# One sequence of lists for the horizontal pass, with the work between them in pieces

## The chip, the core and the metric

The kernel runs on one core of a Trainium2 chip. Five engines work side by side, each from its own queue: TensorE (PE; its weight loads are shown apart as PEld), VectorE (DVE), ScalarE (ACT), GpSimd (POOL), and SyncE (SP), which only issues DMAs here. ScalarE and GpSimd issue DMAs too. The metric is device microseconds of one execution, smaller is better.

## What is computed

The input is an image of 256 channels and 64 x 64 pixels. It goes through a group norm, a linear attention over windows, causal attention with a small feed-forward net, and a layer of experts. The change touches the first part and the layer norm that follows it:

```python
q = sigmoid(Wq x); k = sigmoid(Wk x); v = Wv x     # per pixel; 8 heads of 32
v = v / max(norm(v), 1e-12)
outs = []
for w in (1, 2, 4):
    ws = 64 // w                                   # windows of 64, 32, 16 pixels a side
    wk  = box_sum(k, ws)                           # over the window of each pixel
    wkv = box_sum(outer(k, v), ws)
    attn = einsum('bdhw,bdfhw->bfhw', q, wkv)
    norm = einsum('bdhw,bdhw->bhw', q, wk)
    outs.append(attn / (norm + 1e-6))
x = x + Wout concat(outs) + bout
# then, for the 4096 tokens: layer norm, causal attention, feed-forward net, experts
```

## The kernel before

The windows are not summed. With q and k as keys and queries, each pixel's product with the keys of its window is a masked score, so TensorE computes scores against blocks of 128 keys, a mask (bias) pushes scores outside the window to at most zero, a ReLU drops them, and a second product multiplies by v. The whole is done twice, for groups of four heads (`hg` 0 and 1, function `window_heads`), and in two passes each. The **vertical** pass takes key blocks beside a column strip of the image, the **horizontal** pass key blocks above and below a row strip `Y` (0 to 7; 8 image rows, 512 pixels). Keys wholly inside a window come as sums, not scores: `states` builds them on VectorE, `inside` multiplies them by q on TensorE (L410).

Work comes in **parts**: some rows of a strip times the columns that one key block can reach. `packed` fills **lists** of parts with at most 512 columns, the width of a PSUM buffer, and splits a part between two lists only if at least 96 columns go into the first. Before, each row strip is packed by itself, so its last list may be short.

`push` (one list) is the inner step. It takes four PSUM buffers of six, one for each head; TensorE adds the mask (L349, bf16) and the scores (L358) of every part for the four heads, which lie in four groups of 32 rows of the array. Then four evacuations with a ReLU write `pm` (L327 on ScalarE, L329 on VectorE; of eight in turn, ScalarE takes the 1st, 3rd, 5th, 6th and 8th). Then `add` accumulates the list *before* into `acc` (L391): pm times v. When the last part of a strip and a window size is in, `finish` makes `y`: VectorE adds `ov`, the vertical pass's result, which SyncE loads from memory (L667), and GpSimd multiplies by the inverse norm `rn` (L426); for the smallest window VectorE multiplies alone (L422).

Around the lists of a strip Y stands, behind the list with the index given in the loop's `if`s:

- index 1: `spread_norms`, three products of 32 rows (L474), each copied by ScalarE to `rn` (L477);
- index 2: `boxes(Y + 1)`, GpSimd's window sums for the next strip's norms (L441 to L454);
- index 3: `convolve(Y - 1)`, the output projection of the strip before, twelve matmuls (L505) into two PSUM buffers, each added to the tokens `t` by VectorE (L510);
- second group only, index 4: `measure`, the statistics of four token tiles on VectorE; index 5: `norm`, ScalarE's square root and VectorE's reciprocal and four normalisations; index 7: `turn`, eight transposes (L845), a copy by each of VectorE and ScalarE (L846), and two sums (L847);
- third list from the end: `norms`, three products (L462), ScalarE's copy with the epsilon (L465) and four reciprocals on VectorE (L467).

The order of TensorE and GpSimd is that of the program, by `manual_schedule`. The order of VectorE, ScalarE and SyncE is chosen by the scheduler when the kernel is built, from priorities and its own costs. Behind the second group come the last convolution and norm, the causal attention and the experts, which the change leaves as they are.

Of the kernel before, what the change touches and what calls it, by code (L numbers as in the profile page):

```python
# [19 lines left out]
P = 128  # L20
D = 256
# [83 lines left out]
def packed(parts):  # L105
# [3 lines left out]
    while parts:  # L109
        part = parts.pop(0)  # L110
        if part.size <= room:
            out[-1].append(part)
            room -= part.size
            continue
        rows = room // (part.c1 - part.c0)
        if rows * (part.c1 - part.c0) >= 96:
            first, rest = part.split(rows)
            out[-1].append(first)
            parts.insert(0, rest)
        else:  # L120
            parts.insert(0, part)
        out.append([])
        room = 512
# [54 lines left out]
def window_attention(tc, a, t, eps5, ident, causal, first):  # L178
# [5 lines left out]
    with ExitStack() as ctx:  # L184
# [99 lines left out]
        with tc.manual_schedule(engines={mybir.EngineType.PE}):  # L284
# [3 lines left out]
            causal.measure(7)  # L288
            xns = causal.norm(7, w)
            causal.values(1, psum)  # L290
            causal.values(2, psum)
            causal.turn(7, xns, psum)


def window_heads(tc, a, t, ident, hg, norm, raws, load, psum, pools, tables, consts, late, causal):
# [35 lines left out]
    accs, left, state, ys, waiting = {}, {}, {}, {}, []  # L331

# [72 lines left out]
    def inside(group, acc):  # L405

        wi, Y = group
        for X in range(8):
            for h, hs in enumerate(hss):
                nc.tensor.matmul(  # L410
                    acc.rearrange("p (y x) -> p y x", x=HW)[hs, :, 8 * X : 8 * X + 8],
                    lhsT=state["st"][wi][hs, X, :], rhs=q[hs, 8 * Y : 8 * Y + 8, 8 * X : 8 * X + 8],
# [3 lines left out]
    def finish(group, acc):  # L416
# [3 lines left out]
        rn = state["rn"][wi]  # L420
        if wi == 0:
            nc.vector.tensor_mul(o, acc, rn)  # L422
        else:
            view = lambda s: s.rearrange("p (y b x) -> p y b x", b=8, x=8)
            nc.vector.tensor_add(view(o), view(acc), state["ov"][wi].rearrange("p b (y x) -> p y b x", x=8))  # L425
# [32 lines left out]
    def norms(boxed):  # L458

        pn = psum()  # L460
        for wi, box in enumerate(boxed):
            nc.tensor.matmul(pn[32 * wi : 32 * wi + 32, :], lhsT=sums, rhs=box.rearrange("p y x -> p (y x)"),  # L462
                             start=True, stop=True, skip_group_check=True)
        r = sm.tile([96, 512], F32, name="r", bufs=1)
        nc.scalar.activation(r, pn[0:96, :], AF.Identity, bias=eps6[0:96, :])  # L465
        for j in range(4):
            nc.vector.reciprocal(r[:, j * P : (j + 1) * P], r[:, j * P : (j + 1) * P])  # L467
        return r

    def spread_norms(r):  # L470
        rns = []
        for wi in range(3):
# [6 lines left out]
        return rns  # L479

    def states(Y):


        out = [None]
        for wi in (1, 2):
            n = HALF[wi] // 8
            rows = state["h"].tile([P, 9, 32], F32, name="srows")
            nc.vector.tensor_sub(rows, ikv[:, min(8, Y + n), :, :], ikv[:, max(0, Y - n + 1), :, :])
            st = state["h"].tile([P, 8, 32], F32, name=f"st{wi}")
            if n == 2:  # L490
                nc.vector.tensor_copy(st[:, 0, :], rows[:, 2, :])
                nc.vector.tensor_sub(st[:, 1:7, :], rows[:, 3:9, :], rows[:, 0:6, :])
                nc.vector.tensor_sub(st[:, 7, :], rows[:, 8, :], rows[:, 6, :])
            else:
                nc.vector.tensor_copy(st[:, 0:4, :], rows[:, 4:8, :])
                nc.vector.tensor_sub(st[:, 4:8, :], rows[:, 8:9, :].to_broadcast([P, 4, 32]), rows[:, 1:5, :])
            out.append(st)
        return out

    def convolve(Y):  # L500
        for j in range(2):
            pt = psum()
            for i in range(2):
                for n, wi in enumerate((2, 1, 0)):
                    nc.tensor.matmul(  # L505
                        pt[:, i * D : (i + 1) * D], lhsT=ys[wi, Y][:, (2 * j + i) * P : (2 * j + i + 1) * P],
                        rhs=wo[:, n, :], start=(n == 0), stop=(n == 2),
                    )
            td = t[:, 4 * Y + 2 * j : 4 * Y + 2 * j + 2, :]
            nc.vector.tensor_add(td, td, pt.rearrange("p (i d) -> p i d", i=2))  # L510
# [79 lines left out]
    with tc.manual_schedule(engines={mybir.EngineType.PE, mybir.EngineType.Pool}), ExitStack() as keys:  # L590
        with ExitStack() as vctx:
# [25 lines left out]
            for m in range(4):  # L617
# [9 lines left out]
                kp = turned(m)  # L627
            for m in range(4):
# [24 lines left out]

            for i, parts in enumerate(lists[1:]):
                push(parts)
                if i == len(lists) - 4:
                    r = norms(boxed)
            lists = [packed(part for wi in range(3) for part in above(wi, Y)) for Y in range(8)]
            for each in lists:
                expect(each)  # L660
            push(lists[0][0])
        h = state["h"] = keys.enter_context(tc.tile_pool(name="l0h", bufs=1, side="right", reuse_waits="tile"))
        for Y in range(8):
            ov = [None]
            for wi in (1, 2):
                o = h.tile([P, 8, HW], F32, name=f"ov{wi}")
                nc.sync.dma_start(out=o, in_=oscratch[wi].rearrange("b p (y x) -> y p b x", x=HW)[Y])  # L667
                ov.append(o)
            st = states(Y)
            if hg and Y == 7:  # L670
                causal.load()
            for i, parts in enumerate(lists[Y]):
                if (Y, i) != (0, 0):
                    push(parts)
                if i == 2 and Y < 7:
                    boxed = boxes(Y + 1)
                if i == 1:
                    state.update(st=st, ov=ov, rn=spread_norms(r))
                if i == 3 and Y:
                    convolve(Y - 1)  # L680
                if hg and i == 4 and Y:
                    causal.measure(Y - 1)
# [648 lines left out]
```

## Time and profile before

| | us |
|---|---|
| median of 3 runs | 1993.42 (1993.35 to 1994.79) |
| the profiled execution | 1994.53 |
| its span, first to last instruction | 1992.8 |
| vertical pass, first group | about 91 to 202 |
| horizontal pass, first group | about 202 to 511 |
| vertical pass, second group | about 570 to 682 |
| horizontal pass, second group | about 682 to 1009 |
| causal attention and experts | about 1009 to 1993 |

In a line of the timeline stand: start in us from the span's start, duration in us, engine, line, operation, what is written and what is read, shapes (for a matmul the rows and columns of the array, then the operand), how many instructions are merged into the row, and in brackets the idle time of the engine before it and what ended that. An fp32 matmul is recorded as two passes, so four heads with one part are eight records. In a line of a table by stretches stand: the stretch, its length, the busy time and number of instructions of each engine, the granted clock of TensorE (PEclk, 1 is full), the share of the DMA engines and the GB/s.

### The profile page before, as it was taken

The page shows a single profiled execution, that of the slowest core. Times are in us where ns is not written, and L with a number is a line of the kernel's source. Part 1 is how long each engine was busy: PE and PEld are TensorE (multiplying, and loading weights), DVE is VectorE, ACT ScalarE, POOL GpSimd, SP SyncE. Part 2 cuts the span into 40 slices and gives each one's busy share as a digit, 9 for nine tenths or more (in the row PEclk, how much of TensorE's full clock was granted, in tenths as well). Part 3 has the DMA queues.
Part 4 walks back from the last instruction along what each step waited for, and adds up shares of the span by engine and source line. Part 5 has one row for each costly group of instructions (what it writes and reads, how often), then busy time and mean ns, then how long its engine had stood idle before and what let it go on. Part 6 is the DMA issues. An engine that isn't in the chain of part 4 may idle for free.

```text
span 1992.8 us, 46271 instructions
## 1 busy us (share of the span) xinstructions
PE 1859.6 (93%) x20326; PEld 1218.4 (61%) x20326; DVE 1000.5 (50%) x2190; ACT 777.4 (39%) x1331; POOL 431.8 (22%) x709
## 2 busy tenths in 40 slices
PE   4999999999999999999999999999999999879998
PEld 2655565555665555555575656665666666657777
DVE  4644555544554565555663444554553655443343
ACT  1566444444456644444414233233333234223322
POOL 1384323232155123333110000000000000031220
PEclk9999999999999999999999999999999999879999
DMA  7211100000331100000100000000000000010000
GB/s 242 82 52 45 29 13 18 13 18 12 104 92 40 45 18 18 13 13 13 50 2 0 1 0 1 0 1 0 1 0 1 0 1 0 1 43 22 21 22 22
DMA packets 66890, 53.34 MB, mean 27 GB/s; under 512 B 37568, under 2 KB 56792, under 8 KB 66688
## 3 DMA queue, kind: packets, MB, share of 16 engines
q1 hardware_dynamic: 57296, 31.87, 5.8%
q10 hardware_dynamic: 8128, 14.67, 2.1%
q0 software_dynamic: 1264, 3.84, 0.6%
q8 instruction: 159, 2.61, 0.6%
q14 instruction: 43, 0.35, 0.1%
HBM read 32.93 MB, written 17.44 MB: 25 GB/s over the span
## 4 chain that ended last, share of the span: by engine, by line
PE 42%; DVE 6%; ACT 3%; issue 1%; POOL 0%; ACTq 0%; DVEq 0%; POOLq 0%
PE po L1001 11%; PE pa L957 10%; PE ph L1265 6%; PE py L1285 6%; PE pt L987 2%; PE pm L1058 1%; PE acc L391 1%; PE pm L1068 1%; DVE lnst L704 1%; PE ps L505 1%; DVE sT L990 1%; PE ps L358 1%; DVE nbs L965 1%; PE pm L916 1%; ACT s L970 1%
## 5 line engine op out<-in xcount | busy, mean ns | idle before, releaser
L327 ACT ACTIVATE pm<-ps 128x512 f32<-128x512 f32 (+19 forms) x734 | 362.4, 558 | 348.4 <-issue 194.1
L329 DVE TENSOR_SCALAR pm<-ps 128x512 f32<-128x512 f32 (+23 forms) x442 | 267.6, 636 | 315.7 <-PE ps L358 234.5
L391 PE MATMUL acc<-pm,vh 128*32 128x248 f32 (+22 forms) x3424 | 218.5, 356 | 16.8 <-DVE pm L329 16.7
L358 PE MATMUL ps<-q,kh 32*128 32x248 f32 (+23 forms) x3424 | 204.8, 354 | 0.0
L957 PE MATMUL pa<-k,qT 128*128 128x512 f32 (+3 forms) x416 | 180.2, 574 | 7.1 <-ACT qT L918 5.6
L349 PE MATMUL ps<-table,table 32*128 32x192 bf16 (+19 forms) x2512 | 143.1, 261 | 24.4 <-ACT rn L477 8.4
L990 DVE COPY sT<-pt 128x512 f32<-128x512 f32 (+3 forms) x144 | 92.7, 644 | 142.9 <-PE pt L987 142.7
L391 PEld LDWEIGHTS acc<-pm,vh 128*32 128x32 f32 x3424 | 87.3, 110 | 108.5 <-issue 60.8
L349 PEld LDWEIGHTS <-table 32*128 32x128 bf16 x2512 | 50.0, 92 | 162.5 <-issue 155.7
L358 PEld LDWEIGHTS ps<-q,kh 32*128 32x128 f32 x3424 | 142.6, 188 | 7.3 <-issue 2.5
L426 POOL TENSOR_TENSOR y<-y,rn 128x512 f32<-128x512 f32 x32 | 41.3, 1290 | 449.5 <-DVE y L425 297.9
L959 ACT ACTIVATE s<-pa,v 128x512 f32<-128x512 f32 (+3 forms) x112 | 73.8, 661 | 152.1 <-PE pa L957 151.9
L957 PEld LDWEIGHTS pa<-k,qT 128*128 128x128 f32 x416 | 75.7, 191 | 89.3 <-issue 72.4
L965 DVE TENSOR_REDUCE nbs<-s 128x1 f32<-128x512 f32 (+4 forms) x120 | 77.6, 652 | 80.4 <-ACT s L959 59.1
L1285 PE MATMUL py<-w,hT 128*128 128x256 f32 x512 | 111.8, 379 | 0.0
L1001 PE MATMUL po<-kh,sT 128*128 128x257 f32 x406 | 102.8, 395 | 8.7 <-DVE sT L990 8.5
L1285 PEld LDWEIGHTS py<-w,hT 128*128 128x128 f32 x512 | 97.3, 190 | 15.7 <-issue 1.9
L391 PE MATMUL acc<-pm,v 128*32 128x192 f32 (+11 forms) x1600 | 98.5, 360 | 3.9 <-DVE pm L329 2.4
L358 PE MATMUL ps<-q,k 32*128 32x192 f32 (+11 forms) x1600 | 98.4, 359 | 0.0
L1001 PEld LDWEIGHTS po<-kh,sT 128*128 128x128 f32 x406 | 74.7, 195 | 22.4 <-DVE sT L990 13.2
L505 PE MATMUL ps<-l0wo,y 128*128 128x256 f32 x384 | 87.0, 383 | 0.0
L948 POOL MEMSET s<- 128x32 f32 x20 | 2.5, 124 | 376.4 <-PE pt L987 348.4
(304 smaller groups left out, 2899.0 us busy)
## 6 DMA issues: line engine op xcount, KB each, us to landing
oscratch<-ov ACTq DMA_DIRECT2D x32, 256.0 KB
ov<-oscratch SPq DMA_DIRECT2D x32, 256.0 KB
t<-in_xT SPq DMA_DIRECT2D x32, 128.0 KB
vscratch<-v SPq DMA_DIRECT2D x32, 128.0 KB
vh<-vscratch SPq DMA_DIRECT2D x16, 256.0 KB
raw<-in_x SPq DMA_DIRECT2D x7, 512.0 KB
raw<-in_x ACTq DMA_DIRECT2D x7, 512.0 KB
out<-y SPq DMA_DIRECT2D x7, 512.0 KB
```

Source lines behind the costliest of these rows:

```text
L327: nc.scalar.activation(dst, src, AF.Relu)
L329: nc.vector.tensor_scalar_max(dst, src, 0.0)
L349: nc.tensor.matmul(got[h][:, spot].rearrange("p (y x) -> p y x", y=part.r1 - part.r0), lhsT=spread[hs, int(part.vertical), :], rhs=bias[hs ...
L358: nc.tensor.matmul(got[h][:, spot].rearrange("p (y x) -> p y x", y=part.r1 - part.r0), lhsT=keys[hs], rhs=q[hs, part.r0 : part.r1, part.c0 ...
L391: nc.tensor.matmul(out, lhsT=v, rhs=pm[:, h, spot].rearrange("p (y x) -> p y x", y=part.r1 - part.r0), start=fresh, stop=(left[key] == 0), ...
L505: nc.tensor.matmul(pt[:, i * D : (i + 1) * D], lhsT=ys[wi, Y][:, (2 * j + i) * P : (2 * j + i + 1) * P], rhs=wo[:, n, :], start=(n == 0), ...
L957: nc.tensor.matmul(pp[:, 0:m], lhsT=qTs[g][:, c, i * P - g * 512 : n - g * 512], rhs=x[b // 512][c][:, 0:m], start=(c == 0), stop=(c == DC ...
L965: nc.vector.tensor_reduce(nbs[:, at : at + 1], s[:, b : b + m], AX.X, ALU.max)
L990: nc.vector.tensor_copy(sT[:, 0:full], pt[:, 0:full])
L1001: nc.tensor.matmul(acc, lhsT=sT[0:m, j * P : (j + 1) * P], rhs=rhs, start=(b == 0), stop=(m != P))
L1265: nc.tensor.matmul(ph, lhsT=w1v[:, e, c, f, :], rhs=x2[g][c], start=(c == 0), stop=(c == DC - 1))
L1285: nc.tensor.matmul(py, lhsT=hT[:, e, f, j * P : (j + 1) * P], rhs=w2v[:, e, f, :], start=(e + f == 0), stop=(e == 1 and f == FC - 1))
```

## The change

Six things are changed together.

1. A split of a part is allowed from 40 columns on, not 96. This holds for both passes.
2. The horizontal pass is packed as one sequence over all eight strips, so a list may hold the end of one strip and the start of the next.
3. The work around the lists is cut into pieces, and a table `between` puts one piece (sometimes two) behind each list: of the norms one product step, four single reciprocals and three single spreading products, each behind a list of its own; the window states by window size; the convolution in two halves; statistics and norm in two halves, with the square root as a step of its own (`root`); the transposes by channel half, their sums four lists later (`sum_up`).
4. `turn` copies both halves on ScalarE.
5. VectorE and ScalarE keep program order too, from the first vertical list to the end of the horizontal pass of each group.
6. The norms of strip 0 start eight lists before the end of the vertical pass, not three.

```diff
@@ packed
-        if rows * (part.c1 - part.c0) >= 96:
+        if rows * (part.c1 - part.c0) >= 40:
@@ window_heads: norms, spread_norms -> norms
+    strips = [{"st": [None], "ov": [None], "rn": []} for _ in range(8)]
-    def norms(boxed):
-        pn = psum()
...
-        for j in range(4):
+    def norms(boxed, rns):
+        r = sm.tile([96, 512], F32, name="r", bufs=1)
+        def sum_up():
+            pn = psum()
+            for wi, box in enumerate(boxed):
+                nc.tensor.matmul(pn[32 * wi : 32 * wi + 32, :], lhsT=sums, rhs=box.rearrange("p y x -> p (y x)"),
+                                 start=True, stop=True, skip_group_check=True)
+            nc.scalar.activation(r, pn[0:96, :], AF.Identity, bias=eps6[0:96, :])
+        def invert(j):
             nc.vector.reciprocal(r[:, j * P : (j + 1) * P], r[:, j * P : (j + 1) * P])
-        return r
-    def spread_norms(r):
-        rns = []
-        for wi in range(3):
+        def spread_out(wi):
             pn = psum()
             nc.tensor.matmul(pn, lhsT=spreadh[32 * wi : 32 * wi + 32, :], rhs=r[32 * wi : 32 * wi + 32, :],
                              start=True, stop=True)
             rn = state["h"].tile([P, 512], F32, name=f"rn{wi}")
             nc.scalar.copy(rn, pn)
             rns.append(rn)
+        return [sum_up] + [lambda j=j: invert(j) for j in range(4)], [lambda wi=wi: spread_out(wi) for wi in range(3)]
...
+            keys.enter_context(tc.manual_schedule(engines={mybir.EngineType.DVE, mybir.EngineType.Activation}))
...
+            steps, spreads = norms(boxed, strips[0]["rn"])
             for i, parts in enumerate(lists[1:]):
                 push(parts)
-                if i == len(lists) - 4:
-                    r = norms(boxed)
-            lists = [packed(part for wi in range(3) for part in above(wi, Y)) for Y in range(8)]
-            for each in lists:
-                expect(each)
-            push(lists[0][0])
+                if i >= len(lists) - 9 and steps:
+                    steps.pop(0)()
+            lists = packed(part for Y in range(8) for wi in range(3) for part in above(wi, Y))
+            expect(lists)
+            push(lists[0])
...
+        def plan(at, *tasks):
+            for n, task in enumerate(tasks):
+                between.setdefault(at + n, []).append(task)
+            return at + len(tasks)
...
         for Y in range(8):
+            at, after = firsts[Y], firsts[Y + 1]
+            plan(at, lambda Y=Y: (outer(1, Y), outer(2, Y)))
+            plan(at + 1, *(lambda wi=wi, Y=Y: strips[Y]["st"].append(inner(wi, Y)) for wi in (1, 2)))
+            if Y == 0:
+                plan(at + 1, *spreads)
+            if Y < 7:
+                plan(at, lambda Y=Y: ahead(Y + 1))
+                end = plan(max(after - 5, at + 6), *(lambda n=n, Y=Y: got[Y + 1][0][n]() for n in range(5)))
+                plan(max(end, after + 1), *(lambda n=n, Y=Y: got[Y + 1][1][n]() for n in range(3)))
+            if Y:
+                end = plan(at + 3, *(lambda j=j, Y=Y: convolve(Y - 1, j) for j in range(2)))
+                if hg:
+                    g = Y - 1
+                    end = plan(end, *(lambda j=j, g=g: causal.measure(g, (2 * j, 2 * j + 1)) for j in range(2)))
+                    plan(end - 1, lambda g=g: causal.root(g))
+                    end = plan(end, *(lambda j=j, g=g: xns.update({(g, j): causal.norm(g, w, (2 * j, 2 * j + 1))})
+                                      for j in range(2)))
+                    plan(end, *(lambda c=c, g=g: causal.turn(g, xns[g, 0] + xns[g, 1], psum, c) for c in range(DC)))
+                    plan(end + 4, *(lambda c=c, g=g: causal.sum_up(g, c) for c in range(DC)))
+        if hg:
+            plan(firsts[7], causal.load)
+        for n, parts in enumerate(lists):
+            if n:
+                push(parts)
+            for task in between.pop(n, []):
+                task()
@@ Causal.turn
-            (nc.scalar.copy if c else nc.vector.tensor_copy)(self.x[g][c], pt)
+        self.nc.scalar.copy(self.x[g][c], pt)
```

`firsts[Y]` is the first list whose first part is of strip Y (0, 9, 20, 33, 46, 59, 72, 84; the whole has 93). `outer` issues the two loads of `ov` on SyncE, `ahead` GpSimd's box work, `inner` is one window size of the former `states`.

## The prediction

> **What bounds the kernel now.** First the head of the page: which engine fills the span. Then the busy times of the two horizontal passes (one for each group of four heads), which the change rebuilds. Then the timeline there, list by list.
>
> ```profile
> span 1992.8 us, 46271 instructions
> ...
> PE 1859.6 (93%) x20326; PEld 1218.4 (61%) x20326; DVE 1000.5 (50%) x2190; ACT 777.4 (39%) x1331; POOL 431.8 (22%) x709
> ```
>
> ```profile
> core 0: us, PE busy (x) PEld busy (x) DVE busy (x) ACT busy (x) POOL busy (x), PEclk, DMA share, GB/s
> ...
> 202.00:511.00 309.00, 293.40 (x5579) 178.49 (x5578) 157.38 (x274) 140.22 (x285) 88.35 (x106) 0.99 0.08 18
> ...
> 682.00:1009.00 327.00, 302.81 (x5626) 185.82 (x5618) 195.24 (x385) 145.28 (x298) 87.19 (x101) 0.98 0.09 22
> ```
>
> TensorE is the bound; VectorE is at 51% and 60%, ScalarE at 45%, so neither is a limit by its sum. But a busy TensorE is not one at its peak, so I go by starts of matmuls. An unhindered list:
>
> ```profile
> 996.31 0.40 PE L349 MATMUL ps<-table,table 32*128 32x47 bf16 x12
> ...
> 997.63 1.00 PE L391 MATMUL acc<-pm,vh 128*32 128x141 f32 x16
> ...
> 998.57 0.40 PE L349 MATMUL ps<-table,table 32*128 32x192 bf16 x8
> ...
> 999.76 0.71 PE L391 MATMUL acc<-pm,vh 128*32 128x47 f32 x16
> ```
>
> Bias and scores of two parts with 512 columns take 1.19 us (998.57 to 999.76); 487 columns in three parts, the first of 47, take 1.32 us. Going through all 294 lists of the timeline in this way, an unhindered list costs 1.19 us less 2.1 ns for each column short of 512, plus 0.075 us for each part beyond two; its accumulation 0.14 us plus 1.67 ns a column. So an empty list would still cost about 0.25 us. What exceeds this is stall. Three kinds stand out:
>
> ```profile
> 391.25 3.38 DVE L467 RECIPROCAL r<-r 96x128 f32<-96x128 f32 x4 [1.15 <-ACT r L465]
> ...
> 393.09 0.51 PE L391 MATMUL acc<-pm,vh 128*32 128x189 f32 x4
> ...
> 395.19 0.99 PE L391 MATMUL acc<-pm,vh 128*32 128x189 f32 x12 [1.59 <-DVE pm L329]
> 396.11 0.37 PE L349 MATMUL ps<-table,table 32*128 32x192 bf16 x8
> ```
>
> Four reciprocals run as one block ahead of an evacuation; the accumulation takes 3.02 us (393.09 to 396.11), not 0.93.
>
> ```profile
> 400.24 1.13 PE L474 MATMUL ps<-r,spreadh 32*128 32x512 f32 x6
> ...
> 401.39 1.56 ACT L477 COPY rn<-ps 128x512 f32<-128x512 f32 x3 [1.02 <-PE ps L474]
> ...
> 402.03 0.35 PE L349 MATMUL ps<-table,table 32*128 32x192 bf16 x5 [0.57 <-ACT rn L477]
> ```
>
> Three spreading products take three of six PSUM buffers; the next list waits for ScalarE's copy.
>
> ```profile
> 854.28 0.21 PE L349 MATMUL ps<-table,table 32*128 32x93 bf16 x2
> ...
> 854.53 1.38 DVE L836 TENSOR_SCALAR xn<-t,stats 128x256 f32<-128x256 f32 x4
> ...
> 856.56 0.38 PE L349 MATMUL ps<-table,table 32*128 32x93 bf16 x9 [1.55 <-DVE pm L329]
> ```
>
> In the second group the tokens' norm stands ahead of an evacuation: the list takes 3.52 us, not 1.30.
>
> **What goes.** (a) The reciprocals: 14 accumulations over their price by 1.3, 1.9, 2.8, 2.5, 2.1, 2.6, 2.1 us in the first group and 1.3, 1.9, 2.1, 2.1, 2.9, 3.4, 2.1 in the second: 31.2 us; twice 1.37 us more at the end of the vertical passes: 34 in all. One reciprocal (0.85 us) with one list's evacuations (0.65 or 1.3 us) fits into the list's 2.2 us. (b) The wait behind the spread: 16 x 0.82 = 13.2 us. (c) The norm block: 0.97, 2.22, 2.23, 2.22, 0.95, 2.23, 2.34: 13.2 us. (d) Other lists over their price: 24 us, partly in the wake of (a), partly one-part lists (13 a group; a single part of 329 columns is 0.31 us over) too short to cover ScalarE's two evacuations in a row. Together 85 us.
>
> Part of (a) and (c) is clock. The column PEclk:
>
> ```profile
> 306.00:309.40 3.40, 3.40 (x34) 1.52 (x34) 0.25 (x1) 0.00 (x0) 0.00 (x0) 0.51 0.00 0
> ```
>
> Five such windows (from 306, 350, 811, 883 and 931 us) each follow such a stall within 3 us, and cost about 1.5 us each (the list at 307.6 against the like one at 790.8): 7.5 of the 85 us. [...]
>
> What stays: two of three (ScalarE does a list's first two evacuations in every second list, 1.1 us in a row) still wait. A list after such a one is 0.21 to 0.31 us late where no other TensorE work lies between. By the plan 21 lists of the first group's horizontal pass and 17 of the second's have none: 38 x 0.27 = 10 us. New waits: ScalarE's square root now stands in order behind the statistics, VectorE's y behind its evacuations. Seven strips with 0.3 us would be 2 us; 0.25 us in all 186 horizontal lists would be 46; nothing below zero, since an in-order piece cannot shorten a list. I take 8, nearer the low end, because VectorE is at 60% and a late piece falls mostly on a list in which it has one evacuation. So stalls fall from 85 to 18: **-67 us**.
>
> **What comes.** Packing: the parts go from 100 + 214 to 121 + 242 a group, the lists from 46 + 101 to 45 + 93 (worked out from the rule of the packing; columns unchanged). Parts beyond two in a list rise by 58: x 0.075 x 2 groups = 8.7 us; small first and last pieces some 4 to 5 us more (the 47-column list above is 0.1 over); 9 lists x 0.25 x 2 = -4.5. Together **+9**. [...] 72 evacuations fewer (about 0.17 us fixed cost each, from 0.25 us at 94 and 0.59 at 512 columns) are off the path.
>
> Spreading: three products in three row groups run together, 0.97 us from the accumulation's end to the next bias (the list gap 1.84 us against 0.87 without). One behind each list, each costs that alone, since its neighbours need the same row groups or all rows: 2 x 0.97 x 16 strips = **+31 us**. If the first bias of the next list overlapped it, 25; not below.
>
> Convolution and transposes in two pieces each: one more entry and exit, 0.2 us, x 14 and x 7: **+4**.
>
> Moved at no cost: VectorE's window states (1.2 and 2.0 us) come at the lists that also have a spread, which gives them 3.2 us; without that cover 0.5 us a strip. GpSimd's box work (12 us a strip) starts two lists earlier, behind the product of the last y, and is needed eight lists (about 20 us) later; if it were late, the sums wait for it. SyncE's loads of ov are issued behind the strip's first list, wait as before for the last use of the buffer, and are needed nine lists later; the parameters' 14 loads go ahead of the last pair on that queue, which had 20 us to spare. ScalarE's copy of a spread waits for GpSimd's y product of the strip before, done two lists earlier. The second group's input loads still stand between the last evacuations. Everything after the tokens' layer keeps its order; taking x's copy from VectorE to ScalarE (0.69 against 0.58 us) is off the path.
>
> **Sum.** -67 + 9 + 31 + 4 = -23 us. The profiled execution took 1994.5 us (span 1992.8 and 1.7 around), 1.1 above the median of 1993.4; from the median: 1971.
>
> **Rivals.** *Head-of-line waits* (slower): in program order ScalarE and VectorE must sit out each piece's TensorE product before the next list's evacuation. For it: ScalarE's sequence is now evacuate, wait for the spread or statistics, copy, evacuate. Against: TensorE has the same order, so the piece is done before the next scores. The additions are fixed at 44 us, so beside the 10 us that stay it decides from (85 - 44 - 10)/186 = 0.17 us a list on; at 0.21 us the time is 2001. Chance 0.15. *The evacuation stays the limit*: six PSUM buffers at four a list; (d)'s waits return in most lists after two ScalarE evacuations, also where I count a cover, 0.12 us on average: 1985, 0.20. *Draw*: 0.15 to 0.19 us a list, 1993, 0.08. That the pieces do not land between lists is excluded by the order of the built instructions: one reciprocal between two lists' evacuations.
>
> **Numbers.** Forecast 0.57 (1961 to 1980: from no new waits with packing at 6, to 17 us of them). About 0.2% is what a measurement here can tell from no change. Faster 0.57 + 0.20 = 0.77, same 0.08, slower 0.15. Range 1961 to 1998, which leaves out 0.05 below and 0.13 above.
>
> **What would show it.** Right: no list with over 1 us of stall; single reciprocals between evacuations; spreads at about 0.97 us each, three a strip; half-clock windows in the passes gone; horizontal passes near 302 and 309 us instead of 309 and 327. Wrong: a first horizontal pass of 309 us or more; waits of TensorE for rn or stats; a three-part list that costs no more than one of two parts.

## The result, and the profile after

The changed kernel takes 1963.91 us, the median of four runs (1957.54 to 1964.60), against 1994.11 us of the kernel before in its runs. The ratio is 0.9838 with a 95% interval from 0.9822 to 0.9854: 30 us faster by the medians and 32 by the ratio, where the forecast was 23. The profiled execution took 1963.31 us. Its page says that TensorE is still the bound, now with more matmuls (22286, not 20326) and with less room between them:

```profile
span 1961.6 us, 50126 instructions
...
PE 1867.7 (95%) x22286; PEld 1272.9 (65%) x22286; DVE 1013.5 (52%) x2154; ACT 780.3 (40%) x1295; POOL 438.8 (22%) x709
```

The table by stretches has the two horizontal passes in its first two rows, then the two vertical ones, and last the 3.4 us in which the kernel before ran at half clock (PEclk 0.51). A vertical pass is cut at its first mask product, a horizontal one at the last list ahead of the first spread. The first group's horizontal pass ends where TensorE starts on the second group's projections (2.1 us of idle time ahead of that are in it, 3.1 before), the second's with the last accumulation:

```profile
205.60:504.50 298.90, 295.53 (x6090) 196.41 (x6087) 168.12 (x263) 140.66 (x266) 89.94 (x104) 1.00 0.09 21
672.80:976.90 304.10, 302.74 (x6139) 201.52 (x6135) 196.21 (x363) 148.03 (x284) 88.92 (x99) 1.00 0.10 24
93.00:205.60 112.60, 110.16 (x2593) 73.28 (x2593) 51.15 (x80) 68.39 (x133) 74.32 (x129) 1.00 0.14 48
560.00:672.80 112.80, 110.09 (x2593) 73.33 (x2593) 50.68 (x80) 68.34 (x133) 55.62 (x121) 1.00 0.14 47
306.00:309.40 3.40, 3.28 (x87) 2.36 (x88) 2.72 (x4) 1.69 (x4) 0.00 (x0) 1.00 0.00 0
```

Cut in the same way, the passes of the kernel before are 309.5, 325.4, 113.0 and 113.4 us. The horizontal passes became 10.6 and 21.3 us shorter, the vertical ones 0.5 and 0.6: 33.0 us in all, where the two spans differ by 31.2. So the whole result lies in the passes. No half-clock window is left in the passes (PEclk 1.00; there were five in the horizontal passes).

What TensorE waited for shows it most briefly. The view of waits gives: what waits, what it waits for, us in total, times, the longest. In the kernel before, the rows of the passes were

```profile
PE acc L391 <- DVE pm L329: 19.1, 20, 1.6
...
PE ps L349 <- ACT rn L477: 8.4, 16, 0.6
PE ps L349 <- DVE pm L329: 8.2, 7, 1.6
...
PE ps L349 <- ACT pm L327: 5.2, 21, 0.4
```

that is, 40.9 us for evacuations and for the spread's copy (a wait shows only where the engine is idle). In the changed kernel the same rows are

```profile
PE ps L353 <- DVE pm L332: 0.8, 2, 0.4
...
PE ps L353 <- ACT pm L330: 0.3, 1, 0.3
```

and the wait for `rn` is gone. The reciprocals now stand one by one between two evacuations, here in VectorE's timeline:

```profile
227.78 0.94 DVE L475 RECIPROCAL r<-r 96x128 f32<-96x128 f32 x1
228.88 0.69 DVE L332 TENSOR_SCALAR pm<-ps 128x512 f32<-128x512 f32 x1 [0.16 <-PE ps L362]
229.48 0.94 DVE L475 RECIPROCAL r<-r 96x128 f32<-96x128 f32 x1
231.41 1.28 DVE L332 TENSOR_SCALAR pm<-ps 128x506 f32<-128x506 f32 x2 [0.98 <-PE ps L362]
```

And the price of spreading one at a time, in TensorE's timeline:

```profile
315.45 1.03 PE L395 MATMUL acc<-pm,vh 128*32 128x144 f32 x24
316.41 0.69 PE L479 MATMUL ps<-r,spreadh 32*128 32x512 f32 x1
316.42 0.66 PE L353 MATMUL ps<-table,table 32*128 32x217 bf16 x7
316.94 0.59 PE L479 MATMUL ps<-r,spreadh 32*128 32x512 f32 x1
316.95 0.21 PE L353 MATMUL ps<-table,table 32*128 32x69 bf16 x2
...
317.59 1.14 PE L362 MATMUL ps<-q,kh 32*128 32x217 f32 x19
318.66 1.07 PE L395 MATMUL acc<-pm,vh 128*32 128x155 f32 x24
```

The product's two fp32 passes start at 316.41 and 316.94, and mask products start in between. Most of the scores (19 of 24 records) start only from 317.59 on. From one accumulation's start to the next, lists with a spread are about 0.9 us longer than like ones without, over some 100 lists of this trace.

### The profile page after: what moved, and what is told of

It is laid out like the page before. It is cut to its first block, busy times and chain, and to the rows that moved or that the text cites. A ratio compares the mean times of both kernels' runs of the same rounds, so it can differ in the third digit from the quotient of the medians.

```text
span 1961.6 us, 50126 instructions
## 1 busy us (share of the span) xinstructions
PE 1867.7 (95%) x22286; PEld 1272.9 (65%) x22286; DVE 1013.5 (52%) x2154; ACT 780.3 (40%) x1295; POOL 438.8 (22%) x709
## 4 chain that ended last, share of the span: by engine, by line
PE 43%; DVE 6%; ACT 3%; issue 1%; POOL 0%; ACTq 0%; DVEq 0%; POOLq 0%
PE po L1035 12%; PE pa L991 10%; PE ph L1299 6%; PE py L1319 6%; PE pt L1021 2%; PE pm L1092 1%; PE acc L395 1%; PE pm L1102 1%; PE ps L362 1%; PE ps L507 1%; DVE sT L1024 1%; DVE nbs L999 1%; DVE lnst L731 1%; PE pm L950 1%; ACT s L1004 1%
## 5 line engine op out<-in xcount | busy, mean ns | idle before, releaser
L330 ACT ACTIVATE pm<-ps 128x512 f32<-128x512 f32 (+24 forms) x690 | 358.4, 584 | 330.6 <-PE ps L362 176.8
L332 DVE TENSOR_SCALAR pm<-ps 128x512 f32<-128x512 f32 (+21 forms) x414 | 265.3, 668 | 265.2 <-PE ps L362 172.7
L362 PE MATMUL ps<-q,kh 32*128 32x217 f32 (+27 forms) x3872 | 213.1, 336 | 0.0
L395 PE MATMUL acc<-pm,vh 128*32 128x217 f32 (+27 forms) x3872 | 199.7, 329 | 0.0
L362 PEld LDWEIGHTS ps<-q,kh 32*128 32x128 f32 x3872 | 161.2, 185 | 9.7
L353 PE MATMUL ps<-table,table 32*128 32x184 bf16 (+36 forms) x2904 | 142.7, 245 | 5.4 <-issue 1.2
L395 PEld LDWEIGHTS acc<-pm,vh 128*32 128x32 f32 x3872 | 98.0, 109 | 71.7 <-issue 37.1
L430 POOL TENSOR_TENSOR y<-y,rn 128x512 f32<-128x512 f32 x32 | 40.9, 1277 | 432.8 <-DVE y L429 358.2
L353 PEld LDWEIGHTS <-table 32*128 32x128 bf16 x2904 | 57.0, 92 | 108.4 <-issue 97.6
L362 PE MATMUL ps<-q,k 32*128 32x192 f32 (+30 forms) x1936 | 102.8, 337 | 0.0
L395 PE MATMUL acc<-pm,v 128*32 128x192 f32 (+30 forms) x1936 | 95.9, 326 | 0.6 <-issue 0.6
```

What stands on the lines that cost most here:

```text
L330: nc.scalar.activation(dst, src, AF.Relu)
L332: nc.vector.tensor_scalar_max(dst, src, 0.0)
L353: nc.tensor.matmul(got[h][:, spot].rearrange("p (y x) -> p y x", y=part.r1 - part.r0), lhsT=spread[hs, int(part.vertical), :], rhs=bias[hs ...
L362: nc.tensor.matmul(got[h][:, spot].rearrange("p (y x) -> p y x", y=part.r1 - part.r0), lhsT=keys[hs], rhs=q[hs, part.r0 : part.r1, part.c0 ...
L395: nc.tensor.matmul(out, lhsT=v, rhs=pm[:, h, spot].rearrange("p (y x) -> p y x", y=part.r1 - part.r0), start=fresh, stop=(left[key] == 0), ...
```

## Experiments

All times are medians, the ratio is to the kernel before, with its interval. Single runs of the kernel before range from 1985.44 to 1998.05 us, so the four passes of the profiled execution (vertical and horizontal of the first group, then of the second, cut as above) are the finer measure. They come from one trace of each kernel. Where kernels share a pass's code, some agree in it to 0.2 us (the vertical passes of the kernel before and in program order), others only to 1.1 or 2.6 us (the first of threshold 96 and old packing, the second of the last two rows), so a difference of 1 or 2 us in a sum says little. Stalls "over the price" are a list's time less the list price of the prediction.

| kernel | us | ratio | four passes, us | sum |
|---|---|---|---|---|
| before | 1994.11 | 1 | 113.0 + 309.5 + 113.4 + 325.4 | 861.3 |
| changed | 1963.91 | 0.9838 (0.9822 to 0.9854) | 112.5 + 298.9 + 112.8 + 304.1 | 828.3 |
| reciprocals in a block | 1973.88 | 0.9888 (0.9870 to 0.9907) | 116.4 + 301.9 + 116.4 + 308.4 | 843.1 |
| norms in one step | 1997.89 | 1.0027 (1.0010 to 1.0044) | 115.9 + 304.3 + 117.3 + 324.3 | 861.8 |
| scheduler's order | 2001.20 | 1.0027 (1.0016 to 1.0038) | 117.1 + 305.3 + 117.0 + 324.9 | 864.3 |
| before, program order | 1977.55 | 0.9908 (0.9890 to 0.9926) | 113.0 + 309.7 + 113.5 + 311.6 | 847.8 |
| same, norms earlier | 1971.50 | 0.9895 (0.9873 to 0.9917) | 113.0 + 304.4 + 113.5 + 305.8 | 836.7 |
| same, block apart | 1983.08 | 0.9954 (0.9938 to 0.9970) | 111.4 + 309.5 + 111.9 + 315.4 | 848.2 |
| threshold 96 | 1961.68 | 0.9838 (0.9821 to 0.9855) | 109.7 + 301.7 + 109.4 + 305.8 | 826.6 |
| old packing | 1959.96 | 0.9839 (0.9818 to 0.9860) | 110.8 + 300.6 + 109.8 + 306.1 | 827.3 |
| spreads together | 1949.32 | 0.9773 (0.9755 to 0.9792) | 112.3 + 290.8 + 112.7 + 296.3 | 812.1 |
| evacuations in turn | 1952.12 | 0.9788 (0.9768 to 0.9807) | 110.0 + 295.7 + 110.0 + 302.2 | 817.9 |
| the three together | 1924.98 | 0.9653 (0.9631 to 0.9674) | 106.7 + 285.4 + 109.1 + 291.0 | 792.2 |
| spreads under the convolution | 1914.06 | 0.9616 (0.9591 to 0.9641) | 106.8 + 281.2 + 106.5 + 287.9 | 782.4 |

The theory was the prediction's: stalls went because VectorE's and ScalarE's work comes in pieces between evacuations. The rivals: the program order did it, or the packing with fewer lists did.

**Reciprocals in a block again** (the vertical pass's steps likewise):

```diff
-                end = plan(max(after - 5, at + 6), *(lambda n=n, Y=Y: got[Y + 1][0][n]() for n in range(5)))
+                end = plan(max(after - 5, at + 6), lambda Y=Y: got[Y + 1][0][0](), lambda Y=Y: [got[Y + 1][0][n]() for n in range(1, 5)])
```

> The changed kernel, but the four reciprocals of a strip's norms stand in one piece again, behind one list; everything else stays in pieces and in program order. Theory (pieces): TensorE's stalls went because VectorE no longer has 3.4 to 3.8 us of reciprocals ahead of an evacuation. Then 16 accumulations come 1.3 to 3.4 us late again, on average 2.1 us as in the kernel before: +34 us, about 1998 us (1985 to 2003), with accumulations of 2 to 4 us in the timeline. Rival (order): the program order of VectorE and ScalarE did it, and a block in order is harmless: within 5 us of 1964. Rival (lists): the fewer lists and evacuations did it: within 5 us of 1964.

Measured: 1973.88 us, passes 14.8 us longer. This fits neither theory: the block costs 10 us by the medians and 15 by the passes, not 34. At the end of each vertical pass it costs 3.6 to 3.9 us, but in the horizontal passes only 3.0 and 4.3 us, about half a us a strip. The timeline of VectorE and TensorE says why:

```profile
262.62 3.37 DVE L475 RECIPROCAL r<-r 96x128 f32<-96x128 f32 x4
263.24 1.09 PE L414 MATMUL acc<-q,st 32*32 32x64 f32 x64
264.26 0.99 PE L395 MATMUL acc<-pm,vh 128*32 128x336 f32 x16
```

The block starts right behind VectorE's evacuations, with no wait for `r`, which was ready a list ago, and 1.1 us of products with the window states (L414) run beside it. In the kernel before, in program order, there is neither:

```profile
300.48 1.13 PE L358 MATMUL ps<-q,kh 32*128 32x64 f32 x16
301.13 3.38 DVE L467 RECIPROCAL r<-r 96x128 f32<-96x128 f32 x4 [2.41 <-ACT r L465]
304.44 1.61 DVE L329 TENSOR_SCALAR pm<-ps 128x505 f32<-128x505 f32 x3
305.11 0.31 PE L391 MATMUL acc<-pm,vh 128*32 128x64 f32 x4 [1.22 <-DVE pm L329]
```

VectorE sits idle for ScalarE's copy of the same step (2.41 us), so the block starts only when the next list's scores run, and the evacuations follow at 304.44. So besides its length, a block has a place and a producer.

**The scheduler's order:**

```diff
-            keys.enter_context(tc.manual_schedule(engines={mybir.EngineType.DVE, mybir.EngineType.Activation}))
```

> The changed kernel, but VectorE's and ScalarE's order is left to the scheduler in the passes, as before; the program still has the pieces. In the built order the scheduler puts the four reciprocals back to back in 14 of 16 places and the four normalisations of the tokens in one row again. Theory (pieces): what counts is where the pieces land, so the stalls of the reciprocals (34 us) and of the norm block (up to 13 us) come back: about 2005 us (1990 to 2015). Rival (lists): the packing carries the gain whatever the order of VectorE: within 8 us of 1964.

Measured: 2001.20 us, as the theory of pieces expects, and 0.27% slower than the kernel before. The program still has its pieces; the scheduler puts the reciprocals back together (3.38 us for four in a row, in 14 of 16 places) and the norm in front of evacuations. What the pieces cost stays, and what they gain is gone (passes 864.3 us, not 828.3). So the packing does not carry the gain.

**The kernel before in program order:**

```diff
+            keys.enter_context(tc.manual_schedule(engines={mybir.EngineType.DVE, mybir.EngineType.Activation}))
             for m in range(4):
                 fetch(m)
```

> The kernel before, with nothing changed but that VectorE and ScalarE keep program order from the first vertical list to the end of the horizontal pass. The reciprocals stay in blocks of four, the spreads in threes, the packing as it was. Theory (pieces): the blocks stay and so do their stalls: 1994 us give or take 8. Rival (order): the scheduler's order was at fault, most of the 67 us of stalls go without any of the added costs (44 us): below 1960 us. Rival (head-of-line): pieces behind a TensorE product in order hold the evacuations back: 0.2 us a list, about 2030 us.

Measured: 1977.55 us, passes 13.5 us shorter, between the two theories. All of it is in the second group's horizontal pass (325.4 to 311.6 us); the first group's stays (309.5 and 309.7). The wait of mask products for VectorE (8.2 us in 7 waits before) falls to 0.3: that is the norm of the tokens, which the scheduler had put ahead of evacuations. For this term the order suffices. The reciprocals' waits (19.1 us in 20) stay to the tenth.

**The whole norms step undivided:**

```diff
-                end = plan(max(after - 5, at + 6), *(lambda n=n, Y=Y: got[Y + 1][0][n]() for n in range(5)))
+                end = plan(max(after - 5, at + 6), lambda Y=Y: [f() for f in got[Y + 1][0]])
```

> The changed kernel, but the norms' product, ScalarE's copy and all four reciprocals of a strip stand in one step again, behind one list. A block of four reciprocals behind a list of its own cost only about 10 us (the four passes together 14.8 us). Theory (dependent step): in the kernel before the larger part of each stall is that VectorE, in front of the block, waits for the product and the copy of the same step while evacuations queue up; putting a list between producer and consumer is what gained most. Then this kernel stalls like the one before: 16 times 1.6 to 3.2 us, +30 us over the changed kernel, about 1994 us (1986 to 2000), accumulations late by 1.6 us and more. Rival (block length): the block alone sets the stall and it is cheap in these lists: 1974 us (1970 to 1979), as with the block behind its own list.

Measured: 1997.89 us, within the theory's range, but not in the way it was argued. The first group's horizontal pass is only 5.4 us longer than changed, 2.4 more than with the block alone; 20.2 us are in the second group's. There the block meets the tokens' statistics and norm:

```profile
742.35 3.38 DVE L475 RECIPROCAL r<-r 96x128 f32<-96x128 f32 x4 [1.22 <-ACT r L472]
745.66 0.37 DVE L732 BATCH_NORM_STATS2 lnst<-t 128x6 f32<-128x256 f32 x1
...
746.68 0.61 DVE L332 TENSOR_SCALAR pm<-ps 128x464 f32<-128x464 f32 x1
...
747.35 0.54 PE L353 MATMUL ps<-table,table 32*128 32x320 bf16 x5 [3.44 <-DVE pm L332]
```

VectorE has 4.3 us of other work between two evacuations, TensorE waits 3.44 us, and the transposes wait for `xn` in turn (8.6 us in 5 waits). So here two blocks that meet cost more than both apart (the block behind its own list costs this pass 4.3 us); the changed plan avoids it by giving nearly every list one piece.

**Place and producer, in the kernel before in program order.** First the undivided step two lists earlier:

```diff
-                if i == len(lists[Y]) - 3 and Y < 7:
+                if i == len(lists[Y]) - 5 and Y < 7:
```

> The kernel before in program order (1977.6 us; its horizontal passes 309.7 and 311.6 us), and the undivided norms step of a strip two lists earlier, behind the fifth list from the end. With all four reciprocals and their product in one step the changed kernel's first horizontal pass was only 5.4 us longer than with pieces, though the same block cost about 15 us in the kernel before; there it stood five lists ahead of the strip's end, where products with the window states follow. Theory (place): the block is cheap where 1.1 us of such TensorE work follows: first horizontal pass about 300 us, total about 1960 us (1952 to 1968). Rival (dependent step): VectorE's wait for product and copy makes the stall wherever it stands: 1977 us, give or take 4.

Measured: 1971.50 us, passes 836.7 against 847.8. The horizontal passes are 5.3 and 5.8 us shorter, half of what the theory of place expected: some strips find cover there and some do not. In the lists at 381 and 423 us no stall is left beside the products with the states, in those at 296 and 338 us 1.7 us of it. Then the block behind the list after its product:

```diff
                 if i == len(lists[Y]) - 3 and Y < 7:
                     r = norms(boxed)
+                if i == len(lists[Y]) - 2 and Y < 7:
+                    invert(r)
```

> The kernel before in program order (1977.6 us), the norms' product and copy where they were, and the block of four reciprocals behind the list after it. Theory (dependent step): the block then starts right behind VectorE's last evacuation and not after the wait for ScalarE's copy, some 1.2 us earlier against the next list: 16 x 1.2 = 19 us less, 1958 us (1952 to 1965). Rival (place): behind the next to last list of a strip stand short lists without products with the states, so the block stalls them as before: 1977 us, give or take 5.

Measured: 1983.08 us, no gain; passes 848.2 against 847.8. The expected part is there: the block starts earlier, the stall at the end of a vertical pass falls from 2.69 to 1.13 us, accumulations wait 9.2 us, not 19.1. But mask products now wait 18.8 us for VectorE, not 0.3:

```profile
301.98 3.37 DVE L470 RECIPROCAL r<-r 96x128 f32<-96x128 f32 x4
305.27 0.43 DVE L329 TENSOR_SCALAR pm<-ps 128x329 f32<-128x329 f32 x1
...
307.31 0.28 DVE L498 TENSOR_TENSOR st<-srows 128x128 f32<-128x128 f32 x1
307.52 1.13 DVE L329 TENSOR_SCALAR pm<-ps 128x440 f32<-128x440 f32 x2
...
308.18 0.27 PE L349 MATMUL ps<-table,table 32*128 32x248 bf16 x4 [1.45 <-DVE pm L329]
```

Behind the block, with one small evacuation between, come the window states (305.63 to 307.52), now a second block. The wait moved to the next block on the same engine. The place alone brings 11.1 us in the passes and the producer alone none; the changed kernel has both, and the states in two pieces. How much the states' two pieces are worth by themselves was not tried, nor were the copies of `turn` on ScalarE and the earlier norms of strip 0 (points 4 and 6 of the change).

**The packing.** Threshold 96 in the changed kernel:

```diff
-        if rows * (part.c1 - part.c0) >= 40:
+        if rows * (part.c1 - part.c0) >= 96:
```

> The changed kernel with the split threshold back at 96, so fewer parts (100 + 217 a group, not 121 + 242) in more lists (46 + 97, not 45 + 93). Theory (price of parts): by the list price of the prediction the lists cost 98.3 + 202.4 us a group instead of 100.6 + 203.5: 6.8 us less in the four passes, 1957 us (1952 to 1962). Rival (lists): each list and its four evacuations saved are worth more than two more parts: 10 lists more cost 0.5 us each, 1969 us (1965 to 1974).

Measured: 1961.68 us, passes 1.7 us shorter. The vertical passes go with the price (2.8 and 3.4 us shorter), the horizontal ones the other way (2.8 and 1.7 us longer). Then the old packing altogether, threshold 96 and every strip by itself:

```diff
+            lists = [parts for Y in range(8) for parts in packed(part for wi in range(3) for part in above(wi, Y))]
```

> The changed kernel with the packing of the kernel before (each strip by itself, threshold 96; 46 + 101 lists a group and 100 + 214 parts), everything else as changed. The prediction has the new packing cost 9 us: then 1955 us (1951 to 1959). Theory now: by the list price it cost 3.4 to 7 us, most of it in the vertical passes, and in the horizontal ones the short last lists bring waits for evacuations back: the four passes together within 5 us of the changed kernel, with the vertical passes 3 us shorter each and the horizontal ones 1 to 5 us longer each: 1964 us (1959 to 1970).

Measured: 1959.96 us, passes 1.0 us shorter. "Above and below as one sequence of lists", with 18 lists and 72 evacuations fewer, is worth nothing that these passes can tell: with threshold 96 the sequence leaves the horizontal passes as they are (301.7 and 305.8 us, against 300.6 and 306.1 strip by strip), and the 40-column pieces cost the vertical passes about what the horizontal ones gain.

**The spreads together:**

```diff
-                plan(max(end, after + 1), *(lambda n=n, Y=Y: got[Y + 1][1][n]() for n in range(3)))
+                plan(max(end, after + 1), lambda Y=Y: [f() for f in got[Y + 1][1]])
```

(and likewise for strip 0)

> The changed kernel with a strip's three spreading products and their copies in one step again, behind one list. Theory (row groups): the three run together in 0.97 us, one at a time each costs 0.92 to 1.05 us by the changed trace, so 16 x 2 products less, 32 us; the wait of the next list for ScalarE's copies comes back with 0.8 us x 16 = 13 us: net -19 us, 1945 us (1938 to 1950). Rival (copies in order): with ScalarE in program order three copies of 0.59 us stand ahead of its evacuations, the next two lists are late by 2 us a strip: no gain, 1964 us or more.

Measured: 1949.32 us, passes 16.2 us shorter. The three products run together again, and the wait for the copy is back, no longer than before:

```profile
309.60 1.13 PE L479 MATMUL ps<-r,spreadh 32*128 32x512 f32 x6
310.56 0.24 PE L353 MATMUL ps<-table,table 32*128 32x155 bf16 x3
311.40 0.38 PE L353 MATMUL ps<-table,table 32*128 32x155 bf16 x9 [0.59 <-ACT rn L482]
```

This one piece of the change is a loss: it removed about 0.8 us a strip and paid 1.8 to 1.9, a net 1.0 in the passes.

**ScalarE's evacuations in turn:**

```diff
-        if counter[0] % 8 in (1, 3, 5, 6, 0):
+        if counter[0] % 8 in (1, 3, 5, 7, 0):
```

> The changed kernel, with one digit of the evacuations' pattern changed: in every second list ScalarE takes the first, third and fourth evacuation, not the first, second and fourth. Theory (two in a row): what is left over the price in lists without other work, 10 us in the horizontal and 12 us in the vertical passes, is TensorE waiting for a buffer while ScalarE does two evacuations in a row; released in turn, 10 to 20 us go: 1949 us (1944 to 1955). Rival (price): these are the list price's own errors for odd widths, or the wait moves to the list's end: 1964 us, give or take 4.

Measured: 1952.12 us, passes 10.4 us shorter, at the low end of the theory's gain. The stalls over the price in lists without other work fall by 11 to 12 us, about half. They are hardly seen as idle time; they hide in a mask row that lasts too long. Here is the same list in both kernels. In the changed kernel the fourth head's first mask product starts at 293.17, just after ScalarE's second evacuation in a row has ended (292.55 and 0.57 us):

```profile
292.87 0.66 PE L353 MATMUL ps<-table,table 32*128 32x128 bf16 x11
293.36 0.36 PE L362 MATMUL ps<-q,kh 32*128 32x128 f32 x3
...
292.55 0.57 ACT L330 ACTIVATE pm<-ps 128x485 f32<-128x485 f32 x1
...
293.17 0.21 PE L353 MATMUL ps<-table,table 32*128 32x128 bf16 x1
```

and with evacuations in turn:

```profile
288.09 0.40 PE L353 MATMUL ps<-table,table 32*128 32x128 bf16 x12
288.33 1.18 PE L362 MATMUL ps<-q,kh 32*128 32x128 f32 x24
```

**What helped, together:** spreads together, evacuations in turn, and `>= (96 if part.vertical else 40)`.

> The changed kernel with what helped put together: the three spreading products and copies of a strip in one step, ScalarE's evacuations 1, 3 and 4 of every second list, threshold 96 in the vertical passes and 40 in the horizontal ones. If the gains add up: 16 us for the spreads, 10 us for the pattern and up to 6 us for the vertical threshold in the sum of the passes: 1932 us (1926 to 1940). If the pattern and the vertical threshold remove the same waits, and the spreads' wait for the copy grows with the new pattern: 1942 us or more.

Measured: 1924.98 us, a little below the range: the gains add up (16.2 + 10.4 + 6.2 from 828.3 would be 795.5; the passes are 792.2).

**The spreads under the convolution's cover,** on top of that:

```diff
-                plan(max(end, after + 1), lambda Y=Y: [f() for f in got[Y + 1][1]])
+                plan(max(end, after + 2), lambda Y=Y: [f() for f in got[Y + 1][1]])
-                end = plan(at + 3, *(lambda j=j, Y=Y: convolve(Y - 1, j) for j in range(2)))
+                end = plan(at + 2, *(lambda j=j, Y=Y: convolve(Y - 1, j) for j in range(2)))
```

> The best version so far (1925.0 us; four passes 892.2 us), with the step of three spreading products one list later and the convolution's first half one list earlier, so that both stand behind the same list, spreads first. What is left there are 16 waits of about 0.8 us for ScalarE's copies of the spreads. Theory (cover): twelve convolution matmuls (2.8 us) need one PSUM buffer, so they run while the three copies release theirs: 14 of the 16 waits go, 0.8 x 14 = 11 us: passes 881 us, total about 1914 us (1908 to 1920). Rival (late y): the convolution needs GpSimd's last product of the strip before, which stands behind some 12 us of window sums on GpSimd; one list earlier it is late by a microsecond or more a strip, and the time is 1925 us or more.

Measured: 1914.06 us, 1914 expected; passes 782.4 against 792.2 (the sums of the passes in the expectation, 892.2 and 881, are 100 us too high). Of the 16 waits for the copies 2 are left, both in strip 0, which has no convolution; the convolution itself now waits for VectorE, 1.4 us in 4 waits. In the other strips the convolution covers the copies:

```profile
301.13 1.13 PE L479 MATMUL ps<-r,spreadh 32*128 32x512 f32 x6
302.39 2.83 PE L507 MATMUL ps<-l0wo,y 128*128 128x256 f32 x12
305.15 0.40 PE L353 MATMUL ps<-table,table 32*128 32x217 bf16 x12
```

## Why the prediction was right, point by point

**The stalls: -67 forecast, -65 to -71 measured** over the price in lists without other work: some 91 us before, 72 to 77 of them in the horizontal passes, and 22 to 24 after, 10 of them there. (The lower and the upper figure draw the line between lists with and without other work differently.) No horizontal list with over 1 us of stall is left. Of what stays, the forecast had 10 us from ScalarE's two in a row, which is the size of the horizontal passes' rest; it did not name the rest of 12 to 15 us in the vertical passes. Changing the pattern took half of the whole; what the other half is was not tried. The 8 us of new waits in program order, the head-of-line rival, did not come: 1.1 us of waits for evacuations in all four passes.

The cause was told too simply. The prediction put 34 us on the reciprocals' length; the block alone, in the changed plan, costs 14.8 us in the passes. In the kernel before, put in program order, another place for the whole step takes away 11.1 us, and a list between product and block takes away nothing, because the wait moves to the states' block behind it. So length, producer, place and what stands behind act together; how the 34 us divide among them is not shown. That this term came out right was partly luck: the change altered all of them at once. The norm block (13.2 forecast) was the scheduler's order alone: 13.8 us in the second group's horizontal pass of the kernel before in program order.

**Packing: +9 forecast, +1.0 measured** with the old packing in the changed kernel, and 1 us is within what the passes move by themselves. This step failed, in size. Redone over all lists, the prediction's formula gives 298.0 us a group before and 300.1 after, +4.2 for both: its 8.7 - 4.5. (The 6.8 us that an expectation above has for nearly the same difference do not come out of the formula as it stands.) The other 4 to 5 us came from laying the 0.1 us of one list with a 47-column piece on all small pieces by hand. The rest of the miss is in the horizontal passes, which the formula has 0.6 us longer each and which are 1.7 and 2.0 us shorter than with the old packing. Part of that are waits for ScalarE's evacuations, 2.5 us in 12 with the old packing and its 13 one-part lists a group, 0.3 in 1 with the new one and 3.

The prediction took its row of 1.32 us for a list of three parts. In the vertical passes it was a fair guide: the threshold of 40 costs 2.8 and 3.4 us there. In the horizontal ones 40 is better than 96 by 2.8 and 1.7 us, and over both the measured 1.0 us is far below the forecast of 9. Still, a third part is not free: in the changed kernel a list of 512 columns takes 1.19 us to its accumulation with two parts (at 460.4 us) and 1.39 with three (at 227.3 us).

**Spreading: +31 forecast, 28 to 31 measured:** lists with a spread or a convolution take 33.5 us more over the price, 2.8 of them the convolution's. Undoing it alone won 16.2 us net of a wait that came back with 12 us, together 28.

**Convolution and transposes: +4 forecast, about +4 measured.** From the first matmul to the next instruction, 28 halves of the convolution take 2.79 us each, where 14 wholes took 5.38: 2.8 us. Twelve halves of the transposes at 0.59 us stand for six wholes at 1.02: 1.0 us. The seventh strip's transposes, 1.0 us, now stand behind the last accumulation (at 976.9 us), so that much of the 33.0 us is moved and not saved.

**Sum.** The terms do not simply add, since the stalls that the packing removes are in the first and again in the measured +1.0. With the formula's +4.2 for the packing, and 31 and 3 us for spreading and convolution, -65 to -71 makes -27 to -33; the passes say -33.0, and the forecast said -23. Most of the 10 us between the last two is the packing's miss of 8. The work counted as hidden (window states, GpSimd's boxes, the loads of `ov`) was hidden: TensorE's matmuls waited for none of it. The rival "evacuation stays the limit" (1985) named a true rest, 11 to 12 us by the experiment, but counted it in most lists.

**Clock.** The prediction counted 7.5 us of half clock as removable. All five windows are gone. The two lists that it compares for 1.5 us a window differ by 0.88; the rest is in the accumulation ahead (2.84 us over the price, against 2.09). The length of a wait does not decide: in the kernel before, two waits of 1.22 us (up to 305.3 and 349.3 us) were followed by half clock, two of 1.59 us (up to 395.2 and 439.6) by full clock.

TensorE's busy time in the 3.41 us just ahead does not tell the two apart by itself either. In the kernel before, the five stretches at half clock in the horizontal passes start at 306.04, 350.41, 811.21, 882.89 and 930.68 us and last 3.41 us each. In the 3.41 us ahead of each, TensorE was busy for 1.91, 1.91, 1.54, 1.93 and 1.82 us. In the 3.41 us that end with the wait of 1.59 us up to 395.2 it was busy for 1.82 us as well, and full clock followed. In these rows of the kernel before stand the stretch, its length, the busy time and records of TensorE, its weight loads, VectorE, ScalarE and GpSimd, the clock, the DMA share and GB/s:

```profile
302.63:306.04 3.41, 1.91 (x28) 0.85 (x28) 3.41 (x6) 1.45 (x4) 0.00 (x0) 1.00 0.00 0
306.04:309.45 3.41, 3.41 (x34) 1.48 (x28) 0.21 (x1) 0.00 (x0) 0.00 (x0) 0.50 0.00 0
391.80:395.21 3.41, 1.82 (x36) 0.71 (x24) 3.41 (x6) 1.68 (x5) 0.00 (x0) 1.00 0.00 0
395.21:398.62 3.41, 3.09 (x56) 1.75 (x60) 1.46 (x4) 1.31 (x3) 0.00 (x0) 1.00 0.02 5
```

In the program-order kernel with the earlier step, half clock followed a wait of 2.37 us up to 254.2 us (first row); the list at 296 us, with a stall of 2.0 us, was followed by full clock:

```profile
255.60:259.00 3.40, 3.40 (x92) 2.21 (x88) 1.20 (x2) 1.33 (x3) 1.27 (x1) 0.50 0.07 17
299.50:302.90 3.40, 3.40 (x114) 1.94 (x109) 1.03 (x3) 0.04 (x1) 1.27 (x1) 1.00 0.31 72
```

What decides was not shown.

## What to carry to other kernels

When an engine that drains PSUM also has other work, ask four things of each piece: how long it is, whether its producer stands in the same step, what TensorE has to do beside it, and what stands next on that engine. A fix of one can merely move the wait. Where the program is cut into such pieces, the order must be held too: the scheduler here gathered them again, and the kernel paid for the pieces and gained nothing. Do not cut what runs together: three products in three row groups took 1 us as one step and 2.8 us as three, and their copies could be hidden under a convolution instead.

## What was not expected of the hardware

While a spreading product runs in one group of 32 rows, mask products of the next list start between its two fp32 passes (316.41, 316.42, 316.94 us). Yet this overlap saves little: the list is about 0.9 us longer, where the same two passes take 1.05 us ahead of a convolution (319.67 to 320.72 us), with nothing to overlap.

A wait of about 0.3 us for a PSUM buffer did not show as idle time. It showed as a mask row of 0.66 us (at 292.87 us in the changed kernel) instead of 0.40 (at 288.09 with evacuations in turn). The new pattern of evacuations removed 11 to 12 us of such waits from lists without other work, where the view of waits has 0.3 us for ScalarE's evacuations.

Half clock followed two waits of 1.22 us and did not follow two of 1.59 us, in the same trace; each time it came in the passes of the kernel before, it lasted 3.41 us.
